# One piece for each pair of steps: how a stack of attention layers deals out its side work

## The chip, the cores and the metric

The kernel runs on one core of a Trainium2 chip. The metric is the device time of one execution in microseconds. Five engines work side by side, each with a queue of its own: TensorE (PE in the profile, with PEld for its weight loads), VectorE (DVE), ScalarE (ACT), GpSimd (POOL) and SyncE (SP), which here only issues DMAs. TensorE writes its products to PSUM[...]; VectorE and ScalarE read them there.

## The reference

Four cross-attention layers follow one another on a sequence x of 2048 rows and 256 channels. Each attends to the same 1601 context rows of 512 channels. Layers 0, 2 and 3 ("masked") have 16 heads of 64, a bias on two pairs of token columns, an output bias and a residual; layer 1 ("grouped") normalises its input and has 16 query heads of 16 channels over 4 key heads. All is float32. A masked layer computes, with per-row biases for four token columns in `col_bias`:

```python
q, k, v = hidden @ Wq, ctx @ Wk, ctx @ Wv            # per head of 64
logits = einsum("bhqd,bhkd->bhqk", q, k) * 64 ** -0.5 + col_bias
probs = softmax(logits)
out = (einsum("bhqk,bhkd->bhqd", probs, v)) @ Wo + bo + hidden
```

## The kernel before

**Tiles.** The keys are cut into NT = 13 chunks (twelve of 128 and one of 65), the queries into four parts of 512 columns. A masked layer has eight *blocks* of two heads, the grouped layer four blocks of four heads. A *unit* is one block and one part of the queries, so a block is four units; there are 112 units in all. Each unit takes 13 *steps*, one for each chunk of keys, and the steps of all units run on without a break, two at a time (the loop over `first`, L1073). Two steps are called a *pair* here. As 13 is odd, every other unit begins in the middle of a pair.

**Three units at once.** In a masked layer a step computes scores of the unit at hand (`masked_scores`, L669: two products into one tile `s` of two PSUM banks, a copy to `p` by ScalarE at L687, a running maximum `top` by VectorE at L692). 18 steps later the maximum is subtracted (`subtract`, VectorE, L756, against a PSUM tile `b` that ScalarE fills at L751), the exponential taken (ScalarE, L761) and the sum of exponentials carried on by GpSimd (L766). Two steps after that the product with the values is added up in `po` (L801). So the end of a unit's values falls in step 6 of the unit that is two later, and ScalarE copies it to `oT` (L806).

**PSUM.** Two `s` tiles of two banks each go round among the scores of a pair and three occasional users: the maxima (`maxima`, L728), the denominators (L812) and the projection (L844). One tile `b` has two banks, `po` one, and `pm` one; keys, values and queries of the side work share `pm`.

**Side work.** What a unit needs besides its steps is cut into *pieces* (L27: what to run, a cost, and whether it may not be joined by another). Keys and values of the next block, seven pieces each, wait in a queue (`start_block`, L947). Pieces of a unit have due steps, counted from the step in which they are registered: the queries of the next unit (`query_pieces`, L443), the denominators, their division into `oT` by GpSimd, the projection with the residual (`finish`, L864), and after a layer's last block the store of x, the norm factors or the rows of the output (`after`, L980). `Pieces.steps` (L917) runs what is due in the pair and then takes from the queue as far as a credit allows; the credit grows by a share of the work that is left. A due piece with `shared` set, also one of cost zero such as the division, keeps the queue from being served in that pair. What is still in the queue at the end of a block runs at the start of the next (`flush`, L937). The transposes of `maxima` are emitted at the end of the pair in which a unit has its last step, behind the pieces.

**Order.** Instructions of TensorE, ScalarE and VectorE are tied to the order in which the program emits them (L1126 to L1130). The order on GpSimd and SyncE is free within what data and buffers allow. The sums of exponentials, their reciprocals and the maxima go through DRAM (`on_all_partitions`, L637) to be spread over partitions.

Of the kernel before, what the change touches and what calls it, by code (L numbers as in the profile page):

```python
# [26 lines left out]
Piece = namedtuple("Piece", "run cost shared", defaults=(True,))  # L27
# [7 lines left out]
def tile_cross_attention_stack(ctx: ExitStack, tc: tile.TileContext, t: dict, out: bass.AP):  # L35
# [32 lines left out]
    x, cond = t["x"], t["ctx_2048"]  # L68
    _, S, C = x.shape
    _, T, CT = cond.shape  # L70
# [3 lines left out]
    NB = S // QB  # L74
    QT = QB // P
    TCH = spans(T, P)
    NT = len(TCH)
# [22 lines left out]
    class Scores:  # L100
# [16 lines left out]
        def pair(self, shape=(2, QB)):  # L117
            return self.pairs.tile([P, *shape], FP, name="s")
# [272 lines left out]
    class Masked:  # L391
# [5 lines left out]
        def __init__(self, l):  # L397
            self.l, self.name = l, masked_names[l]
# [44 lines left out]
        def query_pieces(self, unit):  # L443

            xt = unit.transposed_x()

            def queries():
                unit.q = heads.tile([P, QB], FP, name="q", bufs=3)
                pq = ps_m.tile([P, QB], FP, name="pm")
                for k in range(NC):  # L450
                    nc.tensor.matmul(  # L451
                        pq, unit.u.wq[:, k, :], xt[:, k, :], start=(k == 0), stop=(k == NC - 1)
                    )
                nc.scalar.mul(unit.q, pq, 64 ** -0.5)

            return [(7, Piece(queries, 2.0))]

    class Grouped:

# [123 lines left out]
    def keep(l, b):  # L583
        nc.sync.dma_start(out=xT_dram[l][b], in_=xs[:, b])

    def norm_factors(l, b):

        held = {}

        def squares():  # L590
            held["x"] = work.tile([P, NC, QB], FP, name="xT")
            nc.scalar.activation(held["x"], xs[:, b], AF.Square)

        def rms():
            pt = ps_m.tile([P, QT], FP, name="pm")
            for q in range(QT):
                for k in range(NC):
                    nc.tensor.matmul(
                        pt[:, q : q + 1], held["x"][:, k, columns(q)], ones[:, :1],
                        start=(k == 0), stop=(k == NC - 1),  # L600
                    )
            by = small.tile([P, QT], FP, name="rms")
            nc.vector.tensor_scalar(by, pt, 16.0 / C, 16.0 * EPS, ALU.mult, ALU.add)
            nc.scalar.activation(by, by, AF.Sqrt)
            nc.vector.reciprocal(by, by)
            with nc.allow_non_contiguous_dma(reason="512 values, four at a time"):
                nc.sync.dma_start(out=factors[b], in_=by)

        return [
            (9, Piece(lambda: keep(l, b), 0.0)), (9, Piece(squares, 0.0)),  # L610
            (10, Piece(rms, 1.5)),
        ]

    def rows_out(b):

        pt = psum.pair((QT, C))
        for q in range(QT):
            for k in range(NC):
                nc.tensor.transpose(pt[:, q, ts(k, P)], xs[:, b, k, ts(q, P)], ident)
        rows = work.tile([P, QT, C], FP, name="ct", bufs=3)  # L620
        half = QT // 2
        nc.scalar.copy(rows[:, :half, :], pt[:, :half, :])
        nc.vector.tensor_copy(rows[:, half:, :], pt[:, half:, :])
        for q0 in (0, half):
            nc.sync.dma_start(
                out=out[0, b * QB + q0 * P : b * QB + (q0 + half) * P, :].rearrange(
                    "(n p) c -> p n c", p=P
                ),
                in_=rows[:, q0 : q0 + half, :],
            )  # L630

    def columns(q):


        return slice(q, QB, QT)
# [13 lines left out]
    class Unit:  # L649
# [213 lines left out]

        def finish(self):  # L864

            return [
                (3, Piece(self.denominators, 1.0, not self.masked)),
                (5, Piece(self.divide, 0.0)), (8, Piece(self.project, 2.0, False)),
            ]


# [5 lines left out]
    units = []  # L877
# [26 lines left out]
    class Pieces:  # L904

        def __init__(self):
            self.fill, self.later = deque(), deque()
            self.due = {}  # L910
            self.credit = 0.0
# [2 lines left out]
            for steps, piece in found:  # L914
                self.due.setdefault(step + steps, []).append(piece)

        def steps(self, steps, share, cost):  # L917


            self.credit = max(min(self.credit + share - cost, 2.5), -2.5)  # L920
            taken = False
            for step in steps:
                for piece in self.due.pop(step, ()):
                    piece.run()
                    self.credit -= piece.cost
                    taken |= piece.shared
            while self.fill and not taken and self.credit + cost >= self.fill[0].cost / 2:
                piece = self.fill.popleft()
                piece.run()
                self.credit -= piece.cost  # L930
                taken = piece.shared

        def release(self):
            self.fill.extend(self.later)
# [10 lines left out]
    pieces = Pieces()  # L945
# [34 lines left out]
    def after(k):  # L980

        i, b, _ = units[k]
        l, n = blocks[i]
        if n + 1 < layers[l].BLOCKS or not of[k].last:
            return []
        if l + 1 == len(layers):
            return [(9, Piece(lambda: rows_out(b), 1.0))]
        if isinstance(layers[l + 1], Masked):
            return [(9, Piece(lambda: keep(l + 1, b), 0.0))]
        return norm_factors(l + 1, b)  # L990

    DELAY, LAG = 5, 2
# [2 lines left out]
    class Step:  # L995
# [21 lines left out]
                layers[blocks[i + 1][0]].load_wo(made[blocks[i + 1]])  # L1017

        def end(self):
            if self.scoring and self.ca == 5 and self.ka + 1 < len(units):  # L1020
                ahead = unit_of(self.ka + 1)
                pieces.at(self.step - self.ca, ahead.layer.query_pieces(ahead))
            if self.valuing and self.cv == NT - 1:
                k = self.kv
                pieces.at(self.step, self.valuing.finish() + after(k))

                if units[k + 1 : k + 2] and units[k + 1][0] != units[k][0]:
                    pieces.release()

        def share(self):  # L1030

            if self.scoring:
                per_block = NB * len(self.scoring.layer.SUBS)
                i, b, sub = units[self.ka]
                left = per_block - (b * len(self.scoring.layer.SUBS) + sub) - self.ca / NT
                own = 7.0 if self.scoring.masked else 5.0
                spent = 1.0 if self.scoring.masked and self.ca == NT - 1 else 0.0
                return (pieces.left() + own * left) / (NT * left), spent
            return 0.0, 0.0

        def grouped(self, three):

# [27 lines left out]
    def masked(unit):  # L1070
        return unit and unit.masked

    for first in range(0, N + NT + DELAY + LAG + 16, 2):  # L1073
        pair = [Step(first), Step(first + 1)]

        if any(masked(x.scoring) for x in pair):
            if psum.banks:
                psum.by_pairs()
        elif pair[0].exping and not pair[0].exping.masked and not psum.banks:
            psum.singly()  # L1080

        kn, cn = divmod(first + 2 - NT - DELAY, NT)
        ahead = of[kn] if cn == 0 and 0 <= kn < len(units) and of[kn].masked else None
        three = not ahead and not any(masked(x.exping) for x in pair)
        for x in pair:
            x.begin()
        if first == 4:
            token_rows()
        for x in pair:
            if masked(x.exping):  # L1090
                if x.cb == 0 and x is pair[1]:
                    x.exping.maxima_spread()
                x.exping.subtract(x.cb)
        for x in pair:
            if masked(x.scoring):
                x.scoring.masked_scores(x.ca)

        ends = all(masked(x.valuing) for x in pair) and pair[0].cv == NT - 1
        if ends:
            pair[0].valuing.values(NT - 1)  # L1100
        for x in pair:
            if masked(x.exping):
                x.exping.masked_exp(x.cb)
        if ahead:
            ahead.maxima_spread()
        if not ends:
            for x in pair:
                if masked(x.valuing):
                    x.valuing.values(x.cv)
        together = [pair] if masked(pair[0].scoring) and masked(pair[1].exping) else [pair[:1], pair[1:]]  # L1110
        for some in together:
            for x in some:
                x.grouped(three)
                x.end()
            shares = [x.share() for x in some]
            pieces.steps([x.step for x in some], *map(sum, zip(*shares)))
        if ends:
            pair[1].valuing.values(0)
        for x in pair:
            if x.scoring and x.ca == NT - 1:  # L1120
                x.scoring.maxima()


    last = {}
# [39 lines left out]
```

## Time and profile before

| | |
|---|---|
| median of three runs | 4996.74 us (4985.69 to 5004.63) |
| profiled execution, its own time | 4995.41 us |
| its span, first to last instruction | 4993.7 us |
| TensorE busy | 4713.8 us (94%) |
| VectorE busy | 3755.6 us (75%) |
| ScalarE busy | 3214.5 us (64%) |
| GpSimd busy | 2991.6 us (60%) |
| running maximum, one (L692, 128x1024) | 1222 ns |
| subtraction, one (L756, 128x1024) | 1209 ns |
| granted TensorE clock, mean | 0.977 |

A row of the profile has the line of the program, the engine, the operation and the tiles (written <- read). In the list of waits, the numbers are the idle time in all, how often, and the longest. In a view by windows a row has the window, its length, then for PE, PEld, DVE, ACT and POOL the busy time with the number of instructions in brackets, the granted clock, and the DMA share and rate. A row of the timeline has the start, the length, the instructions of the same kind that follow on one another, and in square brackets the idle time of the engine before it with what ended it.

### The profile page before, as it was taken

Reading aid. Unit: us, or ns where it says so; the run is one execution under the profiler, and the core shown is the slowest. Engines: PE = TensorE matmul, PEld = TensorE weight load, DVE = VectorE, ACT = ScalarE, POOL = GpSimd, SP = SyncE. Lnnn points to the kernel's source line nnn. Section 1 sums busy time; section 2 is a strip of 40 time slices with the busy share of each in tenths; the row PEclk is TensorE's granted clock in tenths of the full one; section 3 lists DMA queues with packets and bytes.
Section 4 is the critical chain, followed back from the end, with each engine's and each line's share of the span. In section 5 each row is a group of like instructions: output and inputs, shape, how many; then the busy total and the mean of one; then the engine's idle time right before and its main releaser. Section 6 shows DMA issues by size and latency. Waiting matters only on the chain.

```text
span 4993.7 us, 64038 instructions
## 1 busy us (share of the span) xinstructions
PE 4713.8 (94%) x24004; PEld 2064.5 (41%) x24004; DVE 3755.6 (75%) x3782; ACT 3214.5 (64%) x4000; POOL 2991.6 (60%) x1429
## 2 busy tenths in 40 slices
PE   6899999999999999999999999999999999999986
PEld 4344444434444444454344444444434443444432
DVE  3788888888765565654478888888888888888885
ACT  2676777777634555444567777777777777777774
POOL 1677777787730000000267778777777777778787
PEclk8999999999989999999899999999999999999998
DMA  4222232322201000011133232322223323232211
GB/s 138 55 83 81 80 86 77 84 81 74 78 22 36 19 19 19 26 36 51 32 91 86 81 84 77 81 82 81 74 83 85 82 81 86 75 84 82 75 28 34
DMA packets 352534, 337.88 MB, mean 68 GB/s; under 512 B 120697, under 2 KB 306297, under 8 KB 352224
## 3 DMA queue, kind: packets, MB, share of 16 engines
q1 hardware_dynamic: 348960, 328.41, 23.9%
q8 instruction: 189, 3.10, 0.3%
q0 software_dynamic: 1152, 3.28, 0.2%
q10 hardware_dynamic: 2112, 2.10, 0.1%
q14 instruction: 121, 0.99, 0.1%
HBM read 318.89 MB, written 14.82 MB: 67 GB/s over the span
## 4 chain that ended last, share of the span: by engine, by line
PE 78%; DVE 14%; issue 2%; DMA 2%; POOL 1%; ACT 1%; SPq 0%; another core or an unknown queue 0%; POOLq 0%; DVEq 0%; ACTq 0%
PE po L801 23%; PE s L675 17%; PE t L706 8%; PE pm L381 6%; PE pm L427 5%; DVE p L756 5%; PE s L850 4%; PE pm L451 4%; DVE top L692 3%; PE t L771 3%; PE s L822 2%; DVE xs L862 2%; PE s L735 2%; POOL sums L766 1%; DVE rden L826 1%
## 5 line engine op out<-in xcount | busy, mean ns | idle before, releaser
L766 POOL TENSOR_TENSOR sums<-sums,p 128x1024 f32<-128x1024 f32 (+1 forms) x1152 | 2726.0, 2366 | 662.2 <-ACT p L761 603.7
L687 ACT COPY p<-s 128x1024 f32<-128x1024 f32 (+1 forms) x1248 | 1227.8, 1014 | 744.3 <-PE s L675 693.7
L756 DVE TENSOR_TENSOR p<-p,b 128x1024 f32<-128x1024 f32 (+1 forms) x1248 | 1461.1, 1209 | 77.9 <-ACT b L751 77.9
L801 PE MATMUL po<-p,v 128*64 128x512 f32 (+3 forms) x8320 | 1509.0, 530 | 8.8 <-ACT p L761 7.7
L692 DVE TENSOR_TENSOR top<-s,top 128x1024 f32<-128x1024 f32 (+1 forms) x1056 | 1290.4, 1222 | 251.1 <-ACT p L687 192.7
L675 PE MATMUL s<-q,kT 64*128 64x512 f32 (+1 forms) x4992 | 1318.2, 629 | 73.0 <-DVE top L692 22.9
L761 ACT ACTIVATE p<-p 128x1024 f32<-128x1024 f32 (+1 forms) x1248 | 1255.8, 1059 | 55.1 <-DVE p L756 54.0
L801 PEld LDWEIGHTS po<-p,v 128*64 128x64 f32 (+3 forms) x8320 | 367.3, 126 | 1120.6 <-issue 835.1
L842 POOL TENSOR_TENSOR oT<-oT,by 128x512 f32<-128x512 f32 x112 | 143.3, 1279 | 949.1 <-DMA by<-cols 540.3
L675 PEld LDWEIGHTS s<-q,kT 64*128 64x128 f32 (+1 forms) x4992 | 400.8, 182 | 720.6 <-issue 257.7
L783 ACT ACTIVATE p<-t 128x512 f32<-128x512 f32 (+1 forms) x760 | 412.1, 594 | 413.7 <-PE t L706 372.9
L719 DVE TENSOR_REDUCE row_top<-t 128x1 f32<-128x512 f32 x700 | 450.9, 686 | 261.7 <-PE t L706 256.9
L706 PE MATMUL t<-kT,q 32*128 32x512 f32 (+1 forms) x1880 | 561.4, 641 | 0.0
L771 PE MATMUL t<-q,kT 32*128 32x512 f32 (+1 forms) x1520 | 492.5, 661 | 0.0
L706 PEld LDWEIGHTS t<-kT,q 32*128 32x128 f32 x1880 | 295.1, 316 | 168.0 <-issue 85.7
L381 PEld LDWEIGHTS pm<-wv,ct 128*128 128x128 f32 (+1 forms) x2496 | 292.2, 189 | 98.0 <-issue 54.9
L381 PE MATMUL pm<-wv,ct 128*128 128x128 f32 (+2 forms) x2496 | 320.0, 281 | 10.6 <-DMA ct<-ctxT 4.9
L427 PE MATMUL pm<-ct,wk 128*128 128x256 f32 (+1 forms) x1288 | 296.7, 373 | 1.3 <-DMA wk<-in_L_xattn_Wk_dram 0.8
L427 PEld LDWEIGHTS pm<-ct,wk 128*128 128x128 f32 x1288 | 221.8, 191 | 115.9 <-issue 57.1
L736 DVE TENSOR_REDUCE ntop<-s 128x8 f32<-128x1024 f32 x96 | 117.5, 1224 | 188.9 <-PE s L735 188.9
L850 PE MATMUL s<-oT,wo 128*128 128x512 f32 x392 | 196.6, 624 | 41.5 <-DVE top L690 18.5
L764 POOL COPY sums<-p 128x1024 f32<-128x1024 f32 x96 | 99.5, 1036 | 157.5 <-ACT p L761 157.2
(155 smaller groups left out, 2363.4 us busy)
## 6 DMA issues: line engine op xcount, KB each, us to landing
ct<-ctxT SPq DMA_DIRECT2D x288, 512.0 KB
xT<-xT SPq DMA_DIRECT2D x100, 512.0 KB
spread<-cols SPq DMA_DIRECT2D x96, 512.0 KB
by<-cols SPq DMA_DIRECT2D x192, 128.0 KB
xT<-xs SPq DMA_DIRECT2D x16, 512.0 KB
ct<-ctxT SPq DMA_DIRECT2D x48, 130.0 KB
wk<-in_L_xattn_Wk_dram SPq DMA_DIRECT2D x24, 256.0 KB
wv<-in_L_xattn_Wv_dram SPq DMA_DIRECT2D x24, 256.0 KB
```

Source lines behind the costliest of these rows:

```text
L381: nc.tensor.matmul(pv[:md, d, :f], ct(k)[:, d * P : d * P + md], wv[:, k, :], start=(k == 0), stop=(k == NCT - 1),)
L427: nc.tensor.matmul(pk, u.wk[:, k, :], ct(k), start=(k == 0), stop=(k == NCT - 1))
L675: nc.tensor.matmul(s[:m, h, :], self.u.kT[r, a : a + m], self.q[r, :], start=True, stop=(a != TAIL),)
L687: nc.scalar.copy(p[:m], s[:m])
L692: nc.vector.tensor_tensor(self.top[:m], s[:m], self.top[:m], ALU.max)
L706: nc.tensor.matmul(s[:, at : at + n], self.q[r, columns(q)], self.u.kT[r, a : a + n], start=True, stop=True,)
L719: nc.vector.tensor_reduce(self.top[:, of, q, k : k + 1], s, AX.X, ALU.max)
L756: nc.vector.tensor_tensor(self.p[c][:m], self.p[c][:m], self.less[:m], ALU.add)
L761: nc.scalar.activation(p[:m], p[:m], AF.Exp)
L766: nc.gpsimd.tensor_tensor(self.sums[:m], self.sums[:m], p[:m], ALU.add)
L771: nc.tensor.matmul(s[:m], self.u.kT[r, a : a + m], self.q[r, :], start=True, stop=True)
L801: nc.tensor.matmul(to, v, p, start=(c == 0 and not part), stop=(c == NT - 1 and part != 0))
```

## The change

Pairs in which the unit that scores and the one that takes exponentials are both masked are now served by a function of their own, `pair`. It runs what is due and, if that had no cost, one piece from the queue; only if there are more pieces left than pairs in the block does it take one beside a due piece. A piece of cost zero no longer counts as taken. The other steps keep the credit, with one constant for both kinds of layer.

The due steps change too. The queries of a masked unit, registered in step 7 in place of 5 of the unit before, fall due in its step 11 in place of 7. For the grouped layer they are registered in step 7 and fall due in it. Denominators of masked units come two steps after the end of the values in place of three, projections ten after it in place of eight, and what follows a layer's last block two steps later.

```diff
-            return [(7, Piece(queries, 2.0))]
+            return [(11, Piece(queries, 2.0))]
...
-            (9, Piece(lambda: keep(l, b), 0.0)), (9, Piece(squares, 0.0)),
-            (10, Piece(rms, 1.5)),
+            (11, Piece(lambda: keep(l, b), 0.0)), (11, Piece(squares, 0.0)),
+            (12, Piece(rms, 1.5)),
...
+            last = 10 if self.masked else 8
             return [
-                (3, Piece(self.denominators, 1.0, not self.masked)),
-                (5, Piece(self.divide, 0.0)), (8, Piece(self.project, 2.0, False)),
+                (2 if self.masked else 3, Piece(self.denominators, 1.0, not self.masked)),
+                (5, Piece(self.divide, 0.0)), (last, Piece(self.project, 2.0, False)),
             ]
...
-        def steps(self, steps, share, cost):
-            self.credit = max(min(self.credit + share - cost, 2.5), -2.5)
-            taken = False
+        def own(self, steps):
+            cost, taken = 0.0, False
             for step in steps:
                 for piece in self.due.pop(step, ()):
                     piece.run()
-                    self.credit -= piece.cost
-                    taken |= piece.shared
-            while self.fill and not taken and self.credit + cost >= self.fill[0].cost / 2:
+                    cost += piece.cost
+                    taken |= piece.shared and piece.cost > 0
+            return cost, taken
+
+        def pair(self, steps, pairs):
+            cost, taken = self.own(steps)
+            many = len(self.fill) + len(self.later) > pairs
+            while self.fill and not taken and (many or not cost):
+                piece = self.fill.popleft()
+                piece.run()
+                cost += piece.cost
+                taken = piece.shared and piece.cost > 0
+
+        def steps(self, steps, share):
+            self.credit = max(min(self.credit + share, 2.5), -2.5)
+            cost, taken = self.own(steps)
+            self.credit -= cost
+            while self.fill and not taken and self.credit >= self.fill[0].cost / 2:
                 piece = self.fill.popleft()
                 piece.run()
                 self.credit -= piece.cost
-                taken = piece.shared
+                taken = piece.shared and piece.cost > 0
...
-            return [(9, Piece(lambda: rows_out(b), 1.0))]
+            return [(11, Piece(lambda: rows_out(b), 1.0))]
         if isinstance(layers[l + 1], Masked):
-            return [(9, Piece(lambda: keep(l + 1, b), 0.0))]
+            return [(11, Piece(lambda: keep(l + 1, b), 0.0))]
...
-            if self.scoring and self.ca == 5 and self.ka + 1 < len(units):
+            if self.scoring and self.ca == 7 and self.ka + 1 < len(units):
                 ahead = unit_of(self.ka + 1)
                 pieces.at(self.step - self.ca, ahead.layer.query_pieces(ahead))
...
         def share(self):
             if self.scoring:
-                per_block = NB * len(self.scoring.layer.SUBS)
-                i, b, sub = units[self.ka]
-                left = per_block - (b * len(self.scoring.layer.SUBS) + sub) - self.ca / NT
-                own = 7.0 if self.scoring.masked else 5.0
-                spent = 1.0 if self.scoring.masked and self.ca == NT - 1 else 0.0
-                return (pieces.left() + own * left) / (NT * left), spent
-            return 0.0, 0.0
+                left = self.units_left()
+                return (pieces.left() + 5.0 * left) / (NT * left)
+            return 0.0
...
-        together = [pair] if masked(pair[0].scoring) and masked(pair[1].exping) else [pair[:1], pair[1:]]
-        for some in together:
-            for x in some:
-                x.grouped(three)
-                x.end()
-            shares = [x.share() for x in some]
-            pieces.steps([x.step for x in some], *map(sum, zip(*shares)))
+        together = masked(pair[0].scoring) and masked(pair[1].exping)
+        for x in pair:
+            x.grouped(three)
+            x.end()
+            if not together:
+                pieces.steps([x.step], x.share())
+        if together:
+            pieces.pair([first, first + 1], round(pair[0].units_left() * NT / 2))
```

`units_left` is the old expression for `left`, as a function.

More of the change, by code (lines that the diff above doesn't have):

```diff
@@ L1028, in end, with units_left @@
                     pieces.release()
+        def units_left(self):
+            per_block = NB * len(self.scoring.layer.SUBS)
+            _, b, sub = units[self.ka]
+            return per_block - (b * len(self.scoring.layer.SUBS) + sub) - self.ca / NT
         def share(self):
             if self.scoring:
-                per_block = NB * len(self.scoring.layer.SUBS)
-                i, b, sub = units[self.ka]
-                left = per_block - (b * len(self.scoring.layer.SUBS) + sub) - self.ca / NT
-                own = 7.0 if self.scoring.masked else 5.0
-                spent = 1.0 if self.scoring.masked and self.ca == NT - 1 else 0.0
-                return (pieces.left() + own * left) / (NT * left), spent
-            return 0.0, 0.0
+                left = self.units_left()
+                return (pieces.left() + 5.0 * left) / (NT * left)
+            return 0.0
         def grouped(self, three):
```

## The prediction

> **What bounds the kernel now.** First the busy line of the page, then the list of waits.
>
> ```profile
> PE 4713.8 (94%) x24004; PEld 2064.5 (41%) x24004; DVE 3755.6 (75%) x3782; ACT 3214.5 (64%) x4000; POOL 2991.6 (60%) x1429
> ```
>
> ```profile
> PE s L735 <- DVE top L692: 75.7, 52, 1.8
> ...
> PE s L675 <- DVE xs L862: 22.0, 85, 0.3
> ...
> PE s L675 <- DVE ntop L736: 18.6, 72, 0.3
> ...
> PE s L850 <- DVE top L690: 18.5, 38, 0.5
> ```
>
> TensorE is the bound, and where it stops it waits for VectorE: the maxima transposes for the last running maximum, the scores and the projection for a score tile that VectorE still reads. To see what one pair of steps costs, I cut one block of a masked layer (3038.42 to 3195.53, the fifth of the third layer) at the first score matmul of each pair and asked for the busy time of each window. I name what a pair carries besides its four score and four value products: K keys, V values, Q queries (pieces of cost 2, but for the short tails), D denominators, P projection, M maxima. The count of TensorE instructions tells them apart.
>
> ```profile
> 3050.36:3056.06 5.70, 5.70 (x25) 2.60 (x24) 4.44 (x5) 5.11 (x6) 4.00 (x3) 1.00 0.34 95
> ...
> 3068.59:3072.38 3.79, 3.79 (x18) 1.18 (x17) 3.46 (x4) 2.93 (x4) 2.37 (x1) 1.00 0.29 44
> 3072.38:3079.28 6.90, 6.90 (x36) 3.65 (x34) 4.43 (x4) 5.50 (x7) 3.55 (x2) 1.00 0.25 91
> 3079.28:3086.04 6.76, 6.02 (x21) 1.77 (x21) 5.84 (x5) 3.93 (x4) 6.52 (x4) 1.00 0.36 95
> 3086.04:3092.28 6.24, 5.98 (x26) 2.53 (x25) 5.84 (x5) 4.64 (x5) 6.00 (x4) 1.00 0.03 9
> ...
> 3109.48:3116.10 6.62, 5.23 (x28) 2.22 (x27) 5.26 (x6) 4.13 (x5) 5.41 (x3) 1.00 0.56 129
> ...
> 3182.24:3187.19 4.95, 4.95 (x26) 2.22 (x25) 3.84 (x4) 4.32 (x5) 3.99 (x3) 1.00 0.36 106
> 3187.19:3195.53 8.34, 6.33 (x36) 2.96 (x35) 6.77 (x7) 4.03 (x5) 7.42 (x4) 1.00 0.14 32
> sum 157.11, PE 150.93 PEld 64.62 DVE 131.88 ACT 113.09 POOL 122.54; mean PE 5.81 PEld 2.49 DVE 5.07 ACT 4.35 POOL 4.71
> ```
>
> From top to bottom: K alone (5.70), nothing (3.79), K and M (6.90), P after M (6.76), K after P (6.24), M alone (6.62), D alone (4.95), M and the left-over V tail (8.34). So TensorE's own prices are: bare pair 3.79; K, Q or P 1.91; V 1.98 (a pair with V takes 5.77); D 1.16; M 1.19 (6.90 less 5.71). The timeline shows what the rest is:
>
> ```profile
> 3036.38 1.23 PE L735 MATMUL s<-ident,top 128*128 128x128 f32 x8 [1.76 <-DVE top L692]
> ...
> 3086.04 1.13 PE L675 MATMUL s<-q,kT 64*128 64x512 f32 x4
> 3086.15 1.22 DVE L862 TENSOR_TENSOR xs<-s,xs 128x1024 f32<-128x1024 f32 x1 [0.81 <-PE s L850]
> ...
> 3087.43 1.13 PE L675 MATMUL s<-q,kT 64*128 64x512 f32 x4 [0.26 <-DVE xs L862]
> ```
>
> After P there are two score tiles only; the first score product runs, and the second waits until VectorE has read P's tile. It starts 1.39 after the first instead of 0.86, so the pair is 6.24 and not 5.71: a **handover** of 0.53. The same stands after M (`ntop`) and after D (`rden`), unless another piece follows it on TensorE. And an M with no piece ahead of it waits for VectorE: 1.39 at 3114.94 and 1.76 here.
>
> [...] The trace agrees (1209 to 1225), so the reads of M, D and P can't be short. [...] `top` L692 waits for the copy L687 of the same tile, 192.7 us in all. [...]
>
> **The change, part by part.**
>
> *Pieces per pair.* A block is 26 pairs. It has 7 K and 7 V pieces, and 4 units give 4 Q, 4 P and 4 D: 26 in all. Before, the credit and the zero-cost divide (which counted as taken) gave two pairs with D and a K or V, and the pair after with nothing, and left one V to the flush. After, a pair with its own Q, P or D takes nothing else, since there are never more pieces left than pairs, and each other pair takes one. A unit that starts on a pair (A) and one that starts in the middle (B) give these 13 pairs, f being a K or V: A (0,1) f; (2,3) P; (4,5) f; (6,7) f; (8,9) D; (10,11) Q; (12,0) f M; B (1,2) f; (3,4) P; (5,6) f; (7,8) D; (9,10) f; (11,12) Q M. That is 7 f, as needed.
>
> *TensorE's own work* is unchanged. Per block: 26 x 3.79 = 98.54; 14 f = 6 x 1.91 + 6 x 1.98 + 0.84 + 0.97 (tails: 5.79 less 4.95; 3037.45 to 3038.42) = 25.15; 4 Q and 4 P = 15.28; 4 D = 4.64; 4 M = 4.76. Sum 148.37. The block took 157.11, so 8.7 are waits. I find them in the 26 windows: 8 handovers x 0.53 = 4.2 (after P 4, after M 3, after D 1); P waiting for `top` L690 right after M, 2 x 0.5 = 1.0; M alone 1.39 + 1.76 = 3.15; two Q pairs at 5.85, 0.3. Sum 8.7.
>
> *Removed:* both lone M, since each M now has a piece ahead of it: VectorE ends its last maximum some 5.05 to 5.2 after the pair's start, TensorE comes to M at 5.70. In (12,0) step 0 has no maximum, so VectorE is earlier still. -3.15. P now stands two pairs after M, so it needs only the first maximum of its own pair (2 x 1.21 + 1.22 = 3.64 against P at 3.79): -1.0.
>
> *Added:* every D now stands alone and every M ends its pair, so all 12 of D, M, P are followed by a handover: 12 x 0.53 = 6.36 against 4.24, +2.12. What VectorE is late with next: in A, P's read (to 1.32 into pair (4,5)) meets the copy of `b`, for which VectorE idles 1.15 at 3052.45; its second maximum ends about 1.1 into (6,7), where the second score product is due at 0.86. I take 0.2 for each of the two A units, so +0.1 over the old 0.3. After D, VectorE (1.55 late plus 4.89) is 0.2 late at the next pair but one, under the 0.86.
>
> Per block: -3.15 - 1.0 + 2.12 + 0.1 = **-1.9, taken as -2.0**; new block 155.1. There are 20 such blocks (6, 7 and 7 in the masked layers; the rest start, end or border on the grouped layer): **-40 us**.
>
> *Queries at 11.* Q's result is needed in the next pair. In A that pair's first product is still the old unit's step 12 (0.86), which covers ScalarE's copy (0.07 + 0.60); in B, M (1.19) stands between. Cost nothing; without the cover 0.75 each. The load of xT is registered two steps later, but SP issues it as soon as its buffer is free, a unit ahead, straight after the Q that read it:
>
> ```profile
> 3025.23 0.34 SPq L665 DMA_DIRECT2D xT<-xT  x1
> ...
> 3061.01 0.34 SPq L665 DMA_DIRECT2D xT<-xT  x1
> ```
>
> Nothing. That holds for the grouped layer too, whose queries now fall due in the step that registers them: each load but the first few is issued some 57 us ahead (1706.46 for the queries at 1763.96).
>
> *Denominators at 2* move one pair ahead in B only. D needs POOL's last sum of the unit (the 65-row one in the timeline), which ended 11 to 11.8 before D in B and about 8 before it in A; a pair less leaves over 5. *Divide* stays at 5; POOL's order puts it ahead of the pair's sums and it waits for `by`:
>
> ```profile
> 3075.73 1.28 POOL L842 TENSOR_TENSOR oT<-oT,by 128x512 f32<-128x512 f32 x1 [4.75 <-ACT p L687]
> 3076.96 19.49 POOL L766 TENSOR_TENSOR sums<-sums,p 128x1024 f32<-128x1024 f32 x8
> ```
>
> Behind it stand the sums, and for them the buffers of p (ACT waits for them, 21.3 us in all). POOL has 12 x 2.37 + 1.04 + 1.28 = 30.7 of work in a unit of 39.3, and the empty pair that ran it late goes: nothing, down to -1 per block if those waits reached TensorE. *Projection at 10* gives the divide a pair more.
>
> *Borders.* From layer 0 to the grouped layer, P, the transposed x and the norm factors come two steps later and the queries don't: bounds 0 and 4 x 5; I take +3. In the last block, without fill, VectorE bounds (4.89 a pair and 3.9 a unit): 0, bounds -4 and +4. Credit without the 7.0 in the few unpaired steps: 0, bounds -5 and +5.
>
> Sum: profiled execution 4995.4 (span 4993.7 and 1.7 around it) - 40 + 3 - 2 = 4956; its time is 1.3 under the median of 4996.7, so **4957**. 0.5%, 25 us, is about what a measurement here can tell from no change.
>
> **Rivals.** (1) *The waits come back elsewhere*, time 4988. The twelve handovers are nearer each other: of 13 pairs, six carry an extra read of VectorE, every second. If VectorE's lag isn't gone after one pair, another 0.4 falls on each of four units: 1.6 a block, which leaves -0.4, x 20 = -8. For it: VectorE has 131.88 of busy time in 155. Against: two pairs need 9.8 + 1.3 = 11.1 and last 11.9. (2) *Slower*, time 5025: the read of P just ahead of the copy of `b`. If sub, copy and sub run one after another and the second maximum is 1.7 late in every unit, the second score product waits 0.9, 3.6 a block: -2.0 + 3.6 = +1.6, x 20 = +32. It decides from 0.5 per unit. For it: that copy makes VectorE idle 77.9 us already (93 times). Against: in B, ScalarE copies it a pair ahead, after the exponentials, so half the units don't see it. (3) *More*, time 4930: half of the added handovers hidden and POOL's waits gone, -1.3 a block, -26. (4) *The pieces don't fall as I walk them*: then the windows would keep 3.79 and double pairs, and the time stays, as in (1).
>
> **Chances.** My forecast 0.62, its own range 4942 to 4971; rivals (1) and (4) 0.18 together, 4972 to 5010; (2) 0.12; (3) 0.08. Faster by over 0.5% (under 4972): 0.62 + 0.08 = 0.70, less a little of the forecast's edge, 0.68. Slower: 0.12. Same: 0.20. The range takes the forecast whole, most of (3) and two thirds of (1): 4925 to 4998.
>
> **What would show it.** No window of 3.79 and none over 7 in a regular block; L735 on TensorE no longer waiting for L692; waits of L675 for `rden`, `ntop` and `xs` about 85 to 95 each, 0.26 long; blocks of 155.1. Wrong if `t` or `s` products wait for DMA or POOL, if (6,7) is over 6.2, or if the waits of L675 for L692 grow by over 40 us.

## The result and the profile after

The changed kernel takes 4944.06 us (median of four runs, 4935.98 to 4952.00) against 4991.22 for the kernel before (median of four runs too, three of them those of the table above). The ratio is 0.9903, with a 95% interval of 0.9873 to 0.9932: 34 to 63 us faster, and 47 us by the medians. The forecast was 4957, 40 us under the median then known.

The page's line of busy time, and the list of waits, of the changed kernel (idle time in all, times, longest):

```profile
PE 4747.6 (96%) x24004; PEld 2061.6 (42%) x24004; DVE 3752.7 (76%) x3782; ACT 3218.1 (65%) x4000; POOL 2988.8 (60%) x1429
```

```profile
POOL oT L842 <- DMA by<-cols: 423.6, 10, 76.6
...
PE s L675 <- DVE ntop L736: 23.7, 92, 0.3
PE s L675 <- DVE rden L826: 22.8, 91, 0.3
PE s L675 <- DVE xs L862: 21.9, 85, 0.3
...
PE s L735 <- DVE top L692: 3.1, 2, 1.6
...
PE s L850 <- DVE top L692: 0.5, 2, 0.3
```

Two of these waits as the kernel before had them:

```profile
POOL oT L842 <- DMA by<-cols: 540.3, 49, 72.1
...
PE s L675 <- DVE rden L826: 6.1, 24, 0.3
```

The waits of the maxima for the last running maximum are gone (75.7 us before, 3.1 now), those of the projection too (18.5, now 0.5). In their place stand more handovers: a score product waits behind the read of M (`ntop`) 92 times in place of 72, behind that of D (`rden`) 91 times in place of 24, behind that of P (`xs`) 85 times as before. The division waits for `by` only 10 times, in the grouped layer, just behind it and at the end, in place of 49.

The same block of the third layer as before the change, cut at the first score product of each pair (window, length, then PE, PEld, DVE, ACT and POOL busy with their instructions, granted clock, DMA):

```profile
3019.24:3025.48 6.24, 5.98 (x25) 2.53 (x25) 6.06 (x6) 3.93 (x4) 4.73 (x3) 1.00 0.56 155
3025.48:3031.18 5.70, 5.70 (x21) 1.85 (x21) 3.36 (x3) 4.20 (x5) 4.67 (x3) 1.00 0.37 107
3031.18:3037.42 6.24, 5.98 (x26) 2.53 (x25) 4.88 (x5) 3.75 (x5) 3.27 (x2) 1.00 0.01 3
3037.42:3043.53 6.11, 6.11 (x26) 2.44 (x25) 6.01 (x6) 5.95 (x9) 4.48 (x3) 1.00 0.32 86
3043.53:3048.47 4.94, 4.94 (x26) 2.21 (x24) 4.37 (x4) 3.71 (x4) 4.31 (x3) 1.00 0.38 106
3048.47:3054.70 6.23, 5.97 (x21) 1.77 (x20) 5.98 (x7) 4.04 (x5) 5.54 (x3) 1.00 0.06 16
3054.70:3061.53 6.83, 6.83 (x36) 3.75 (x35) 3.50 (x4) 4.79 (x6) 6.75 (x4) 1.00 0.31 101
...
3090.00:3096.92 6.92, 6.92 (x32) 2.90 (x31) 5.52 (x5) 4.84 (x7) 6.84 (x4) 1.00 0.52 146
...
sum 155.63, PE 152.53 PEld 64.52 DVE 131.72 ACT 113.25 POOL 122.44; mean PE 5.87 PEld 2.48 DVE 5.07 ACT 4.36 POOL 4.71
```

The first seven rows are the pairs of a unit A, in the order that the prediction walked out: f, P, f, f, D, Q, f M. Each pair behind an M, a P or a D is 6.24; the pair (6,7), fourth row, is 6.11; the eighth row is B's last pair, Q and M, with TensorE busy throughout. There is no pair of 3.79 and none over 7, here or in the other 19 regular blocks. The block takes 155.63 where it took 157.11.

TensorE's busy time went up by 33.8 us although its work is the same. The rows show where most of that comes from: a pair with one K and a handover counts 5.98 us as busy, and the same pair without the handover 5.71. About half of each handover of 0.53 is booked as busy time and half as idle time, so a higher busy share is not by itself progress.

To see where the 43.4 us between the two spans lie, all runs below are cut into the same four stretches: up to the end of the first block; the 20 regular blocks; the border with the grouped layer between them; and the last block with the drain behind it, in which no scores are left. Times are microseconds, worked out from the first score product after each fourth set of maxima.

| kernel | first | 20 blocks (each) | grouped layer, borders | last | span |
|---|---|---|---|---|---|
| before | 250.2 | 3146.1 (157.31) | 1372.6 | 224.8 | 4993.7 |
| after | 243.6 | 3113.2 (155.66) | 1375.2 | 218.2 | 4950.3 |

So 32.9 us come from the regular blocks, 6.6 from the last stretch and 6.6 from the first; the middle gives 2.6 back. The first stretch tells nothing about the change: its first score product starts at 78.4 us before and at 69.4 after, 9 us apart, ahead of all side work that the change moves. In the middle stretch the granted clock differs from run to run (0.94 to 0.96 around the grouped layer in the three runs compared below). In the last one it differs too, 0.92 before and 0.93 after, and 0.89 to 0.94 in the runs below; more on that further down.

### The profile page after: what moved, and what is told of

The parts are those of the page before. It is cut to its first block, busy times and chain, and to the rows that moved or that the text cites. A ratio compares the mean times of both kernels' runs of the same rounds, so it can differ in the third digit from the quotient of the medians.

```text
span 4950.3 us, 64060 instructions
## 1 busy us (share of the span) xinstructions
PE 4747.6 (96%) x24004; PEld 2061.6 (42%) x24004; DVE 3752.7 (76%) x3782; ACT 3218.1 (65%) x4000; POOL 2988.8 (60%) x1429
## 4 chain that ended last, share of the span: by engine, by line
PE 85%; DVE 10%; issue 1%; POOL 1%; ACT 1%; DMA 1%; SPq 0%; POOLq 0%; DVEq 0%; ACTq 0%
PE po L801 27%; PE s L675 19%; PE t L706 8%; PE pm L381 6%; PE pm L427 6%; PE s L850 4%; PE pm L451 4%; PE t L771 3%; DVE rden L826 2%; DVE ntop L736 2%; PE s L822 2%; DVE xs L862 2%; PE s L735 2%; DVE top L692 1%; DVE p L756 1%
## 5 line engine op out<-in xcount | busy, mean ns | idle before, releaser
L692 DVE TENSOR_TENSOR top<-s,top 128x1024 f32<-128x1024 f32 (+1 forms) x1056 | 1290.6, 1222 | 233.0 <-ACT p L687 169.6
L675 PE MATMUL s<-q,kT 64*128 64x512 f32 (+1 forms) x4992 | 1348.5, 634 | 91.8 <-DVE ntop L736 23.7
L675 PEld LDWEIGHTS s<-q,kT 64*128 64x128 f32 (+1 forms) x4992 | 390.6, 182 | 741.8 <-issue 210.2
L736 DVE TENSOR_REDUCE ntop<-s 128x8 f32<-128x1024 f32 x96 | 117.5, 1224 | 229.0 <-PE s L735 229.0
L427 PEld LDWEIGHTS pm<-ct,wk 128*128 128x128 f32 x1288 | 221.0, 190 | 150.0 <-issue 93.6
L850 PE MATMUL s<-oT,wo 128*128 128x512 f32 x392 | 199.6, 632 | 17.5 <-POOL oT L842 13.6
```

Source lines behind the costliest of these rows:

```text
L427: nc.tensor.matmul(pk, u.wk[:, k, :], ct(k), start=(k == 0), stop=(k == NCT - 1))
L675: nc.tensor.matmul(s[:m, h, :], self.u.kT[r, a : a + m], self.q[r, :], start=True, stop=(a != TAIL),)
L692: nc.vector.tensor_tensor(self.top[:m], s[:m], self.top[:m], ALU.max)
```

## The experiments

Ten more kernels were measured. "Theory of the terms" is the sum of the prediction: TensorE's own work, a handover where nothing covers it, the waits of M and P. Ratios are to the kernel before, on the same chip.

**The new rule alone, the new due steps alone.** The first kernel keeps `pair` and sets every due step back; the second keeps the credit and takes only the new due steps.

```diff
 # pair_only, against after
-            return [(11, Piece(queries, 2.0))]
+            return [(7, Piece(queries, 2.0))]
-            last = 10 if self.masked else 8
+            last = 8
-                (2 if self.masked else 3, Piece(self.denominators, 1.0, not self.masked)),
+                (3, Piece(self.denominators, 1.0, not self.masked)),
-            if self.scoring and self.ca == 7 and self.ka + 1 < len(units):
+            if self.scoring and self.ca == 5 and self.ka + 1 < len(units):
 # and 11, 11, 12, 11, 11 back to 9, 9, 10, 9, 9 in norm_factors and after
```

> The new rule (one piece a pair) with the old due steps: queries at 7, denominators 3, projections 8 after the end of the values. The order becomes A: P f f Q D f fM; B: P f f Q D fM. Theory of the terms (TensorE's own work 148.4 a block, 0.53 for each handover not covered, the waits of P and M for VectorE): no lone M, but P stands right behind M as before (0.5 in B), 12 handovers: block 156.0, against 157.3 before and 155.7 with the whole change; the run about 25 us faster than before. Rival (the even spread of pieces alone makes the gain): block 155.7 or less, the whole gain of 47 us.

> The old rule (credit) with the new due steps. The order becomes uneven: per four units two pairs carry nothing and two or three carry D and a K or V. Theory of the terms: Q ahead of every M in B, so no lone M that waits; P two pairs behind M; a piece behind D covers its handover in three of four units, 9 handovers in place of 12; an empty pair ahead of P makes it wait about 0.5 twice: block 155.0, as fast as the whole change or a little faster, 40 to 55 us under before. Rival (the even spread makes the gain): with empty and double pairs left, the block stays at 157 and the time at that of before.

| kernel | ratio (95%) | median us | each of 20 blocks | last |
|---|---|---|---|---|
| pair_only | 1.0005 (0.9997 to 1.0013) | 4991.83 | 158.04 | 228.4 |
| due_only | 0.9928 (0.9915 to 0.9942) | 4954.03 | 155.98 | 218.0 |

The new rule alone gains nothing; its blocks are 0.7 longer than before. The new due steps alone give 36 of the 47 us, although their order still has empty and double pairs. The 11 us between them and the whole change lie within the two intervals. (The blocks and the last stretch of `pair_only` are 18 us longer than before, and its time still did not rise: its profiled execution makes them up in the first and the middle stretch, 236.9 and 1361.2. In the first the clock was 0.96 against 0.92 before; whether that is the reason in all 13 runs is not shown.) Both theories were wrong on `pair_only`, from which 25 and 47 us were expected; on `due_only` the rival was wrong, and the theory of the terms near: 36 us where it had 40 to 55. Windows of `pair_only`:

```profile
3086.01:3090.96 4.95, 4.95 (x26) 2.22 (x25) 4.12 (x4) 4.32 (x5) 4.28 (x3) 1.00 0.35 106
3090.96:3098.43 7.47, 6.49 (x36) 3.11 (x35) 6.00 (x6) 4.18 (x6) 6.55 (x4) 1.00 0.21 43
...
3170.16:3177.62 7.46, 6.47 (x35) 2.99 (x34) 6.00 (x6) 4.22 (x6) 6.55 (x4) 1.00 0.20 52
sum 158.05, PE 152.53 PEld 64.68 DVE 131.90 ACT 113.20 POOL 122.47; mean PE 5.87 PEld 2.49 DVE 5.07 ACT 4.35 POOL 4.71
```

Here D stands alone and the next pair carries a piece and M. In these two rows the piece is the short tail (65 keys), so TensorE comes to M early and waits 0.7 for the running maximum, which VectorE ends late since D's read came first. I had priced these pairs at 7.43 with a full piece and then taken off 1.0 for each tail. The tails' shortness is worth nothing there: 156.0 and twice 1.0 make the 158.0. Windows of `due_only`:

```profile
3017.78:3022.09 4.31, 4.05 (x17) 1.09 (x16) 4.13 (x4) 2.70 (x3) 3.21 (x2) 1.00 0.43 123
3022.09:3028.10 6.01, 5.75 (x23) 1.85 (x21) 5.20 (x5) 5.05 (x6) 5.43 (x3) 1.00 0.27 87
...
3040.45:3047.12 6.67, 6.67 (x35) 3.57 (x33) 5.96 (x7) 3.83 (x4) 5.96 (x3) 1.00 0.28 79
3047.12:3052.82 5.70, 5.70 (x22) 1.85 (x21) 5.38 (x5) 4.20 (x5) 2.36 (x1) 1.00 0.51 136
```

A pair with nothing but a handover (4.31), P waiting 0.26 behind it (6.01), then D with a K (6.67) and no handover behind it (5.70). D, K and Q together are 12.37 here; the whole change pays 4.94 + 6.23 for D and Q, and 1.91 or more for the K in another pair, 13.08. One block of this run took 162.1 and is in the mean; 13 of the 20 take 155.4, 0.25 less than those of the whole change. Unevenness as such costs nothing here.

**Which due step.** Three kernels take the whole change and set back one due step each.

```diff
 # queries7
-            return [(11, Piece(queries, 2.0))]
+            return [(7, Piece(queries, 2.0))]
 # project8 (with 9, 9, 10, 9, 9 in norm_factors and after)
-            last = 10 if self.masked else 8
+            last = 8
 # den3
-                (2 if self.masked else 3, Piece(self.denominators, 1.0, not self.masked)),
+                (3, Piece(self.denominators, 1.0, not self.masked)),
```

> The whole change, but the queries of masked units fall due in step 7 again. In B they then share a pair with D (order A: f P f Q D f fM; B: f P f QD f fM, and in the last unit of a block QD, nothing, M). Theory of the terms: one M per block is alone again, behind an empty pair and the D whose read VectorE still owes, and waits about 2; the other pairs keep their terms: block 158.5, 55 to 60 us slower than the whole change, that is a little slower than the kernel before. Rival (the place of Q costs nothing, since its result is ready in either): block 155.7.

> The whole change, but the projection (and what follows a layer's last block) at its old step, 8 after the end of the values. Theory of the terms: P right behind M waits 0.5 for the running maximum in B, and (6,7) in A gets back to 5.85 from 6.11, since P's read no longer meets the copy of b: +0.25 in two units, block 156.2, 10 us slower than the whole change. Rival (the place of P doesn't matter, VectorE only has to do the read some time): block 155.7, no difference.

> The whole change, but the denominators three steps after the end of the values, as before: B becomes f P f f D QM. Theory of the terms: the same 12 handovers in another order (D's now falls on the pair with Q and M), so block 155.7 to 155.9, no difference. Rival (D's earlier step is what keeps VectorE's read away from M): M waits about 0.7 in B, block 157, 25 us slower.

| kernel | ratio (95%) | median us | each of 20 blocks | last |
|---|---|---|---|---|
| queries7 | 1.0005 (0.9995 to 1.0014) | 4987.96 | 158.18 | 220.0 |
| project8 | 0.9928 (0.9915 to 0.9942) | 4952.08 | 156.25 | 226.4 |
| den3 | 0.9907 (0.9890 to 0.9923) | 4941.84 | 155.70 | 217.3 |

All three came out as the theory of the terms had them, to 0.4 us a block. With the queries at 7 the whole gain is gone: 2.5 a block, most of it at the block's end. Windows of `queries7`, the last three pairs of a block (Q and D; nothing; M alone):

```profile
3157.25:3163.91 6.66, 6.66 (x30) 2.97 (x29) 5.34 (x5) 5.26 (x8) 5.11 (x3) 1.00 0.40 118
3163.91:3168.88 4.97, 4.12 (x18) 1.08 (x17) 4.78 (x5) 3.37 (x4) 2.60 (x2) 1.00 0.43 109
3168.88:3176.09 7.21, 5.45 (x27) 2.14 (x27) 5.84 (x5) 4.48 (x5) 7.13 (x4) 1.00 0.12 34
```

In the last row M waits 1.56 for VectorE, and score products at the row's start wait 0.8 in two parts. In the whole run the waits of M are back at 39.1 us. The projection's step is worth 0.6 a block (P right behind M is 6.76 again) or 12 us in the 20 blocks; the distance to the whole change is 8 us by the medians and 12 by the ratios, 10 expected. Its last stretch is 8 us longer as well, but at a lower clock (0.89 against 0.93). The denominators' step is worth nothing.

**The handovers, taken away.** The next kernel is the whole change, with the piece of the six pairs behind an M, P or D emitted ahead of the scores.

```diff
+    FRONT = (0, 4, 10, 1, 5, 9)
...
+        together = masked(pair[0].scoring) and masked(pair[1].exping)
+        early = together and pair[0].ca in FRONT
+        if early:
+            pieces.pair([first, first + 1], round(pair[0].units_left() * NT / 2))
         for x in pair:
             if masked(x.scoring):
                 x.scoring.masked_scores(x.ca)
...
-        if together:
+        if together and not early:
             pieces.pair([first, first + 1], round(pair[0].units_left() * NT / 2))
```

> The whole change, but in the pairs that follow a D, a P or an M the piece (K, V or Q) is emitted ahead of the pair's scores in place of behind its value products. The work is the same. Theory of the terms: the piece takes 1.9 on TensorE while VectorE reads the tile for 1.3, so all 12 handovers of 0.53 go (6.4 a block), while the pair behind the copy of b loses 0.4 more in each A unit: block about 150.1, 20 blocks x 5.5 = 110 us faster than the whole change, about 4835. Rival (VectorE is the real bound and its waits come back elsewhere): running maxima end later by the 1.9 that the scores are late, the next pair's scores wait for them, block 154 or more.

The ratio is 0.9857 (0.9842 to 0.9872), 4919.41 us, and a block 153.89. It is faster than the whole change by about 25 us, and not by 110. The waits of this kernel:

```profile
PE s L675 <- DVE top L692: 68.3, 204, 2.6
PE s L850 <- DVE top L692: 34.5, 87, 0.5
PE s L822 <- DVE top L692: 23.2, 48, 0.5
```

The handovers to `ntop`, `rden` and `xs` have left the head of the list, and what came is the rival's wait: P and D (L850, L822) wait for the running maximum that holds the first score tile, and so do score products. An early piece puts the scores 1.9 later, and with them the maximum. Where the next pair carries P or D, they have to wait. Windows of the same kernel, from a pair with P (a K of the next pair at its end) on:

```profile
3016.37:3024.15 7.78, 7.46 (x30) 3.36 (x28) 6.87 (x7) 5.06 (x6) 7.10 (x3) 1.00 0.32 106
3024.15:3028.46 4.31, 3.86 (x18) 1.18 (x17) 3.10 (x3) 3.55 (x5) 2.35 (x1) 1.00 0.41 122
3028.46:3034.79 6.33, 6.13 (x25) 2.44 (x25) 6.18 (x6) 6.09 (x8) 4.49 (x3) 1.00 0.01 3
3034.79:3041.46 6.67, 6.67 (x31) 2.82 (x29) 5.96 (x7) 3.83 (x4) 5.97 (x3) 1.00 0.28 79
3041.46:3045.24 3.78, 3.78 (x17) 1.17 (x17) 3.47 (x4) 3.15 (x4) 2.36 (x1) 1.00 0.33 75
```

The last two rows are D and an early Q, and the rest of Q's pair: 10.45 in place of 4.94 + 6.23 = 11.17, so 0.72 was won there. Row three, the pair behind the copy of `b`, is 6.33.

Two kernels follow from this. One has the early piece only behind D, the other frees the first score tile sooner: in the pairs with P, and with D in B, VectorE takes the second subtraction behind the first maximum.

```diff
 # early_d
-    FRONT = (0, 4, 10, 1, 5, 9)
+    FRONT = (9, 10)
 # early_sub, against early_piece
+    LATE = (2, 3, 7)
...
         for x in pair:
-            if masked(x.exping):
+            if masked(x.exping) and not (late and x is pair[1]):
...
                 x.scoring.masked_scores(x.ca)
+            if late and x is pair[0]:
+                pair[1].exping.subtract(pair[1].cb)
```

with `late` true in unmixed pairs whose `pair[0].ca` is in LATE.

> As the run with early pieces, but only in the pairs behind a D: (10,11) in A and (9,10) in B. What stands in the trace of that run: where the next pair holds P or D, the early piece makes the running maximum late and P or D waits 0.3 to 0.5 for the first score tile, so those pairs won nothing. Theory: only the four pairs behind D win, 4 x 0.53: block 153.5, the same time as the run with all pieces early, within 10 us. Rival (each early piece wins a part): block 154.7 to 155, half of the gain gone.

> As the run with all pieces early, and in the pairs with a P, and with a D in B, VectorE takes the subtraction of the second step behind the first running maximum in place of ahead of it. VectorE's work is the same; the first score tile, which P and D wait for, comes free 1.2 earlier. Theory: the waits of P and D (0.48, 0.32 and 0.49 in two units) go, 2.6 a block; the pair behind the copy of b in A takes 0.4 back: block 151.3 to 152.1, 35 to 50 us faster than the run with all pieces early. Rival (VectorE is full there, so any order ends as late): block 153.8.

| kernel | ratio (95%) | median us | each of 20 blocks |
|---|---|---|---|
| early_d | 0.9852 (0.9836 to 0.9869) | 4911.66 | 154.37 |
| early_sub | 0.9822 (0.9806 to 0.9839) | 4896.86 | 152.59 |

`early_d` has about the time of all early pieces (4911.66 against 4919.41), but its blocks are longer than the 153.5 expected: the two pairs behind A's D won 0.72 each, those behind B's D nothing. There the piece is the tail of K or of V, and the pair behind it, Q and M, takes 7.29 in place of 6.92 with two waits of a score product for L692. What its blocks lose against `early_piece` it gets back elsewhere: its middle stretch is 1366.6 against 1385.6, and 12.4 of that lie in the first block behind the grouped layer (231.1 against 243.5). `early_sub` cut the block by 1.3, where 1.8 to 2.6 were expected: the waits of L850 for L692 left the list of waits, those of L822 fell from 23.2 to 1.2, and those of the score products grew from 68.3 to 84.0. So of 57.7 us of waits at P and D, 56.5 went and 15.7 came back as idle time at the scores; the rival (VectorE is full, any order ends as late) expected no change.

**The tails.** Both short pieces lay in a pair that VectorE bounds, as in `pair_only`: in `early_sub` TensorE is idle for 0.12 in the row of D that ends with a short piece (3049.22 to 3055.45, 6.23 with 6.11 busy) and for 0.60 in the one behind it (4.73 with 4.13 busy). The last two kernels take the short piece first; the second has the late subtraction only in the pairs with P.

```diff
+            order = [NT - 1, *range(0, NT - 1, 2)]
-            loads.extend(lambda c=c: context_slice(c, held) for c in range(0, NT, 2))
-            return [Piece(lambda c=c: piece(c), cost(c)) for c in range(0, NT, 2)]
+            loads.extend(lambda c=c: context_slice(c, held) for c in order)
+            return [Piece(lambda c=c: piece(c), cost(c)) for c in order]
 # tail_first_b also
-    LATE = (2, 3, 7)
+    LATE = (2, 3)
```

> The early pieces with the late subtraction, and the short tail piece (65 keys) of keys and of values taken first in place of last. In the runs so far both tails lie behind D in B, in a pair that VectorE bounds, so that their shortness on TensorE is lost: there TensorE waited 0.1 to 0.6 for running maxima in the two pairs after. First in the queue they lie at the start of a block's K and V, behind M, where VectorE has one maximum less to take. Theory: the waits of those pairs go, about 1.0 for each of the two tails: block 150.6 to 151.6, 20 to 40 us faster than the run with the tails last. Rival (VectorE's work in two units is the bound by now, wherever the short piece lies): block 152.6.

> As the run with the tails first, but the late subtraction in the pairs with P alone, no longer in B's pair with D. Theory: D waits 0.49 again in each B unit, and the pair behind it gets back some 0.3 of it, since VectorE no longer idles ahead of its first maximum: block 0.4 slower, 151.0 to 152.0. Rival (the late subtraction only shifts the wait by a pair): no difference to the other run.

| kernel | ratio (95%) | median us | each of 20 blocks |
|---|---|---|---|
| tail_first | 0.9754 (0.9733 to 0.9774) | 4862.15 | 150.83 |
| tail_first_b | 0.9761 (0.9742 to 0.9779) | 4863.66 | 151.01 |

As expected, 1.8 a block for the place of two half-length pieces. The two kernels don't differ beyond their intervals; the 0.2 a block between them is half of what was expected. The list of waits of `tail_first_b` has D's wait back (23.0 us) and the scores waiting 47.8 us for L692 in place of 59.5. The waits that are left in `tail_first`:

```profile
PE s L675 <- DVE top L692: 59.5, 180, 2.1
...
PE s L735 <- DVE top L692: 2.7, 4, 1.6
```

The first is 60 us in the whole run, and each block is 2.5 over the 148.37 of TensorE's own work. This version is faster than both kernels: 2.5% under the one before.

## Why the prediction was right

**The order of pieces and TensorE's own work.** Right: the windows follow the walk pair by pair, and the price list (3.79, 1.91, 1.98, 1.16, 1.19) gives each row of the whole change to 0.1, handovers, (6,7) and the short piece of K (5.35, where it gives 5.16) apart. One flaw of the list stayed hidden. A D that shares its pair with a K or V costs less than the list says: 6.68 and 6.73 in the block before, where the list has 6.86 and 6.93. (The short K was priced from such a pair, hence the 5.16.)

```profile
3061.91:3068.59 6.68, 6.68 (x34) 3.58 (x32) 5.27 (x7) 4.02 (x5) 6.01 (x3) 1.00 0.22 78
...
3140.24:3146.97 6.73, 6.73 (x42) 4.00 (x40) 5.33 (x7) 4.01 (x5) 6.04 (x4) 1.00 0.33 100
```

The prediction's sum of waits still closed at 8.7, because the two pairs with a lone M cost 0.35 more than prices, handover and M's wait add up to (6.62 against 6.37, 8.34 against 8.24), and that cancels the 0.38 of the two pairs with D. The change takes away both, so the forecast of the block came out unharmed; that is luck.

**The waits removed.** Right, in place and size: M's 75.7 us and P's 18.5 us went. `queries7` and `project8` show which due step removed them: the queries' step, which puts a piece ahead of every M in B, and the projection's, which takes P away from M. Rival (1), waits that come back elsewhere, did not come: score products wait for L692 for 18.5 us in all, 22.9 before. No kernel has the queries' step alone.

**The handovers added.** Right: 92, 91 and 85 of them, 0.26 long in the list and 0.53 in the pair. That this term is a real wait for VectorE and no part of TensorE's work is shown by the early Q behind D, where it went (in `early_piece` the waits behind `rden` are 0.5 us in place of 22.8). That all of them could be had, which was expected of `early_piece` and not part of the prediction, was wrong. One read took 1224 ns for M (L736), 1224 for D (L826) and 1225 for P (L862, 128x1024) in the kernel before; that they can't be short, as the prediction has it, was not shown: no other form of them was tried.

**The pair behind the copy of `b`.** The term was under-sized. The prediction took 0.2 for (6,7) in each of the two A units; it is 0.4 where the pair carries a K (6.11 less 5.71) and 0.34 where it carries a V (6.11 less 5.77). That is 0.34 a block, and most of the distance between the -1.93 that the prediction's terms add up to and the -1.48 by which the block shown here changed. (The mean of the 20 blocks changed by 1.65, as some blocks of the kernel before took longer than 157.11; with it the blocks gave 33 us in place of 40.) That P's read ahead of the copy is the cause is borne out by `project8`, where the same two pairs are back at 5.87 and 5.92:

```profile
3021.49:3027.36 5.87, 5.87 (x26) 2.53 (x25) 5.77 (x6) 4.99 (x8) 3.70 (x3) 1.00 0.31 89
3099.56:3105.48 5.92, 5.92 (x33) 2.95 (x33) 5.75 (x6) 4.95 (x7) 3.63 (x3) 1.00 0.31 91
```

Rival (2) had this wait in every unit at 0.9; in B the pair behind the copy shows nothing but P's handover.

**Queries, loads, denominators, division.** Costs of nothing, borne out. The queries' move has no price in the rows with Q (6.23 with its handover, 6.92 with M), and SP still issues the load of xT right behind the Q that frees its buffer:

```profile
3018.39 0.34 SPq L665 DMA_DIRECT2D xT<-xT  x1
...
3054.80 0.34 SPq L665 DMA_DIRECT2D xT<-xT  x1
```

Q ran on TensorE from 3016.38. The division's wait of 4.75 on POOL is gone too; GpSimd now has it behind the pair's sums (start, length, no idle time ahead of it):

```profile
3057.98 1.28 POOL L842 TENSOR_TENSOR oT<-oT,by 128x512 f32<-128x512 f32 x1
3059.21 4.80 POOL L766 TENSOR_TENSOR sums<-sums,p 128x1024 f32<-128x1024 f32 x2
```

ScalarE's waits for buffers of p did not fall with it (21.3 us before, 42.5 after), and no gain on TensorE is seen from it.

**Borders.** Two of the terms were wrong. The last block was put at 0 with bounds of 4 either way; the last stretch gained 6.6. It goes with the projection's step and what hangs on it: the three kernels with the projection at 8 have 224.8, 226.4 and 228.4 there, the nine with it at 10 have 215.8 to 221.0, in one profiled execution each. The granted clock does not go with it: `project8` has 226.4 at 0.89, but `due_only` has 218.0 at 0.91 and the kernel before 224.8 at 0.92. How the later step saves the time stays open. One wait that looks like the cause does not explain it, that of P for the division. The lines are those of the kernel before, of the changed one and of `project8`:

```profile
PE s L850 <- POOL oT L842: 17.4, 4, 9.4
...
PE s L850 <- POOL oT L842: 13.6, 2, 9.0
...
PE s L850 <- POOL oT L842: 13.5, 2, 9.3
```

`project8` waits there no longer than the whole change, yet its last stretch is the longer one. The +3 for the border between layer 0 and the grouped layer can't be told from the changes of the clock there (0.94 before, 0.95 after, 0.96 in `project8`). The -2 in the prediction's sum has no working in its text; it should not have been there. That the total came out near the forecast is in part luck, since these terms hide each other: the blocks gave 7 us less than forecast and the last stretch 6.6 more.

**What the change's name says** is not what made it faster. One piece for each pair, alone, gave nothing, and in the blocks it lost 0.7 each; the prediction, which priced the parts together, did not see this.

## What to carry to other kernels

Where one engine is nearly always busy (TensorE 94% of the span before, 96% after), price a pair of steps from the profile as the sum of its own pieces, and then look for the few places where the second engine's read holds a buffer. What decided here was what stood on TensorE between that read (1.22 us) and the next user of the buffer: with nothing there the handover cost 0.53, with a K behind D none (the 5.70 of `due_only`). Evenness of the load was worth nothing by itself here (a ratio of 1.0005), and two short pieces gave 1.8 us a block once they were moved out of pairs in which TensorE waited for VectorE. Change one due step at a time: of the three set back here, one takes the whole gain with it, one some 8 to 12 us, one nothing, and the rule that gave the change its name won nothing by itself.

## What the runs showed that was not expected

Moving a piece ahead of the scores won 0.72 where the wait it covers was 0.53: the pair D, then Q took 6.67 + 3.78 in place of 4.94 + 6.23. The other 0.19 does not come from the early place. `due_only` has the same 6.67 for D with a K at its usual place, 0.19 less than the price list's 3.79 + 1.16 + 1.91 = 6.86; the pairs of D with a full piece in the other kernels are as cheap, and the change, which leaves D alone, gives that up. Why it is cheaper was not tried.

The place of two pieces of half length in a block of 26 pairs was worth 1.8 us a block, more than the whole change (1.65).
